# Values projected once and brought by DMA, masks cut to two of three key blocks, and paired score banks in a windowed attention

## The chip, the cores and the metric

The kernel runs on one core of a Trainium2 chip. The metric is the device time of one launch in microseconds (us); less is better. A core has five engines with queues of their own: TensorE (PE, with its weight loads shown apart as PEld), VectorE (DVE), ScalarE (ACT), GpSimd (POOL) and SyncE (SP), which here issues DMAs. Engines wait for each other through semaphores, and each works through its own queue in order.

## The reference, cut to what matters

The input is `x` of 4 x 1024 tokens with 128 features, in float32. Two adaLN blocks follow each other. Block 0 is a linear attention and a mixture of 16 experts. Block 1 begins with the attention that is changed here, and ends with two layers of local attention (8 heads of 64) with a gated MLP.

```python
# block 1, first attention: 16 heads of 8, window 64, 16 prefix keys
qkv = x @ w_qkv.T; q, k, v = split(qkv)          # heads of 8
sg = einsum(q, k[:16]) * scale                    # global prefix keys, causal
st = einsum(q, k_window) * scale                  # keys in (q_pos-64, q_pos], without the prefix
scores = concat(where(mg, sg, -1e9), where(mt, st, -1e9))
out = softmax(scores) @ concat(v[:16], v_window)
x = x + ga * (out @ w_out.T)
# block 0, the experts that are touched too
h = silu(xf @ w1) * (xf @ w3);  y = einsum(h, w2, comb)
```

## The kernel before, in words

Tokens are worked on feature-major: `hT[b]` holds the normed input of batch `b` as 128 features x 1024 tokens. Three stages follow each other: block 0 (to about 316 us of the profile), the windowed attention (316 to 577 us), and the two local layers (577 us to the end). PE runs in the order in which the program writes its matmuls; the order on DVE, ACT and POOL is made by a scheduler when the program is built, and each of them then follows its list. The program divides PSUM into eight banks of 512 floats per partition: four with the tag `s`, two with `t`, one with `m`, one with `o`.

The windowed attention takes 32 tiles of 128 queries (4 batches x 8). A tile is four chunks of 32 queries; each chunk has three blocks of 32 keys (its own and the two before it) and 16 prefix keys, so 112 keys for each of 16 heads. The heads go in four groups `j` of four.

- `scores(b, t)` (L249) fills four `s` banks, one for each `j`: a matmul of an identity with the mask table opens each bank (L255, 448 columns), 16 matmuls add the window's scores (L261), four add the prefix keys (L270). Float32 matmuls run as two instructions, so L261 has 32 for a tile and L270 has 8.
- `weights(b, t)` (L715): for each `j` a maximum (`maximum`, L279 on DVE); for `j` = 0, 1, 2 DVE subtracts it (L724) and ACT takes the exponential (L725); for `j` = 3 four ACT instructions read the bank with the maximum as bias (L728).
- `flip(b, t, js)` (L730) transposes the weights of two `j` on PE into the two `t` banks (L735); ACT copies them out (L737).
- `values(b, t)` (L694): POOL lays the windows of `hT` side by side (L701 to L707), PE projects the values of each of the four chunks' 112 keys (L710, 8 instructions into the `m` bank), and ACT copies them out (L713).
- `outputs(b, t)` (L741) multiplies weights and values into the bank `obank` (L752, 128 instructions); DVE divides by the sum (L754, L756). `back` (L759) turns the result on PE (L762) into the free end of `obank`, and ACT copies it (L765).
- `project_out` (L767), `queries` (L220), `keys` (L228), `tokens` and `normed` (the norms before and after, L773 and L782) come in some tiles only, and use the `m` bank.

One loop over `g` from -1 to 33 holds the written order. For one `g`:

```python
when(g + 2, scores)
when(g + 2, weights)
# queries (b+1) at t = 2, 4; tokens or normed in some g
when(g - 1, back)
when(g + 1, flip, (0, 1)); when(g + 1, values)
when(g, outputs); when(g + 1, flip, (2, 3))
# project_out at g % 4 == 1; keys (b+1) at t = 3, 5; project (first local layer) in the last six
```

All weights of the local layers and the rotary table are loaded at the stage's start (L606 to L615). In block 0, `hidden` (L483) makes two matmuls into two `s` banks, ACT's Silu reads the first (L492), POOL multiplies by the routing weight (L494), DVE multiplies with the second (L496).

Of the kernel before, what the change touches and what calls it, by code (L numbers as in the profile page):

```python
# [19 lines left out]
F32 = mybir.dt.float32  # L20
BF16 = mybir.dt.bfloat16
AF = mybir.ActivationFunctionType
# [4 lines left out]
P = 128  # L27
# [21 lines left out]
def adaln_blocks(ctx: ExitStack, tc: tile.TileContext, a: dict, out: bass.AP):  # L49
# [199 lines left out]
    def scores(b, t):  # L249
        nt = f"{b}_{t}"  # L250
        q1, kx, kg = kept1[b, "q"], kept1[b, "kx"], kept1[b, "kg"]
        S = [ps.tile([P, 512], F32, tag="s", name=f"s_{nt}_{j}", bufs=4) for j in range(4)]
        sv = [x[:, 0 : 4 * (W3 + PREFIX)].rearrange("p (h k) -> p h k", h=4) for x in S]
        for j in range(4):
            pe.matmul(sv[j], lhsT=identb, rhs=mks[:, min(t, 1), :].unsqueeze(1).to_broadcast([P, 4, W3 + PREFIX]), start=True, stop=False)  # L255
        for a in range(4):
            i = 4 * t + a
            lo = max(0, 2 - i)
            for j in range(4):
                rw = slice(32 * j, 32 * j + 32)  # L260
                pe.matmul(  # L261
                    sv[j][32 * a : 32 * a + 32, :, lo * KB : W3].rearrange("p h (c k) -> p h c k", k=KB),
                    lhsT=q1[rw, i * KB : (i + 1) * KB],
                    rhs=kx[rw, i - 2 + lo : i + 1].rearrange("p c h k -> p h c k"),
                    start=False,
                    stop=False,
                )
        for j in range(4):
            rw = slice(32 * j, 32 * j + 32)
            pe.matmul(sv[j][:, :, W3:], lhsT=q1[rw, t * P : (t + 1) * P], rhs=kg[rw, 4 * j : 4 * j + 4, :], start=False, stop=True)  # L270
        mx = pre.tile([P, H0], F32, tag="mx", name=f"mx_{nt}", bufs=3)
        kept1[b, t, "s"] = sv, mx
        if (b, t) == (0, 0):
            for j in range(4):
                maximum(b, t, j)

    def maximum(b, t, j):
        sv, mx = kept1[b, t, "s"]
        dve.tensor_reduce(mx[:, 4 * j : 4 * j + 4], sv[j], AX.X, ALU.max, negate=True)  # L279

    s_attn = float((8.0**0.5) ** -0.25)
    gabo = const("gabo", [P, B])
    with (
# [12 lines left out]
        def blk(k):  # L298
            return slice(k * BLK, (k + 1) * BLK)
# [170 lines left out]
        def shared_hidden(b):  # L470

            hh = []
            for i in range(2):
                h = ps.tile([P, BLK], F32, tag="s", name=f"hs{i}_{b}", bufs=4)
                for k in range(NB):
                    pe.matmul(h[k * INTER : (k + 1) * INTER, :], lhsT=ws13[:, i, :], rhs=hT[b][:, blk(k)], start=True, stop=True)
                hh.append(h)
            u = wp.tile([P, BLK], F32, tag="u", name=f"us_{b}")
            act.activation(u, hh[0], AF.Silu)
            g = kept[b, "gs"] = wb.tile([P, BLK], F32, tag="gs", name=f"gs_{b}")  # L480
            dve.tensor_tensor(g, u, hh[1], ALU.mult)

        def hidden(b, k, c):  # L483

            nm = f"{b}_{k}_{c}"
            hh = []
            for w in (w1, w3):
                h = ps.tile([P, BLK], F32, tag="s", name=f"h_{nm}", bufs=4)
                pe.matmul(h, lhsT=w[:, c * P : (c + 1) * P], rhs=hT[b][:, blk(k)], start=True, stop=True)  # L489
                hh.append(h)  # L490
            u = wp.tile([P, BLK], F32, tag="u", name=f"u_{nm}")
            act.activation(u, hh[0], AF.Silu)  # L492
            kept["u"] = u
            pool.tensor_tensor(u, u, kept[b, k, "cw"][:, c, :], ALU.mult)  # L494
            g = kept[b, k, c, "g"] = wp.tile([P, BLK], F32, tag="g", name=f"g_{nm}", bufs=4)
            dve.tensor_tensor(g, u, hh[1], ALU.mult)  # L496

# [104 lines left out]

    wl = []
    for l in range(DEPTH):
        w = [const1(f"wqkv_{l}", [P, 3, HEADS * DH]), const1(f"wo_{l}", [P, 4, D]), const1(f"w1_{l}", [P, 2 * HID]), const1(f"w2_{l}", [P, 3, D])]
        nc.sync.dma_start(out=w[0], in_=a["wqkv"][l].rearrange("p (i c) -> p i c", i=3))  # L606
        nc.sync.dma_start(out=w[1], in_=a["wo"][l].rearrange("(c p) d -> p c d", p=P))
        nc.sync.dma_start(out=w[2], in_=a["mw1"][l])
        for j, r in enumerate(CH):
            nc.sync.dma_start(out=w[3][:r, j, :], in_=a["mw2"][l][j * P : j * P + r, :])  # L610
        wl.append(w)

    abs_ = [const1(f"ab_{l}", [P, 2, NT, 2, DH]) for l in range(DEPTH)]
    tab = abs_[DEPTH - 1]
    nc.sync.dma_start(out=tab, in_=a["tab"])  # L615

# [68 lines left out]
    m = mods[1]  # L685
    with (
        tc.tile_pool(name="w6o", bufs=1) as wo6,
        tc.tile_pool(name="w6b", bufs=2) as wb,
        tc.tile_pool(name="w6", bufs=3) as wp,
        tc.manual_schedule(engines={mybir.EngineType.PE}),  # L690
    ):
        odd.append(wo6)

        def values(b, t):  # L694

            nt = f"{b}_{t}"
            hr = wp.tile([P, 4, KV], F32, tag="hr", name=f"hr_{nt}", bufs=2)
            c0 = 2 if t == 0 else 0
            win = hT[b][:, (4 * t + c0 - 2) * KB :]
            win = bass.AP(tensor=win.tensor, offset=win.offset, ap=[win.ap[0], [KB, 4 - c0], [1, W3]])  # L700
            pool.tensor_copy(hr[:, c0:, 0:W3], win)  # L701
            if t == 0:

                pool.memset(hr[:, 0:2, 0 : 2 * KB], 0.0)
                pool.tensor_copy(hr[:, 0, 2 * KB : W3], hT[b][:, 0:KB])
                pool.tensor_copy(hr[:, 1, KB:W3], hT[b][:, 0 : 2 * KB])
            pool.tensor_copy(hr[:, :, W3:], hT[b][:, 0:PREFIX].unsqueeze(1).to_broadcast([P, 4, PREFIX]))  # L707
            vp = ps.tile([P, 4, D], F32, tag="m", name=f"vp_{nt}")[0:KV]
            for c in range(4):
                pe.matmul(vp[:, c, :], lhsT=hr[:, c, :], rhs=wqkv1[:, 2, :], start=True, stop=True)  # L710
            v = kept1[b, t, "v"] = wp.tile([KV, 4 * H0, 9], F32, tag="vb", name=f"vb_{nt}")
            pool.memset(v[:, :, 8:9], 1.0)
            act.copy(v[:, :, 0:8], vp.rearrange("p c (h e) -> p (c h) e", e=8))  # L713

        def weights(b, t):  # L715

            sv, mx = kept1[b, t, "s"]
            for j in range(4):
                if (b, t) != (0, 0):
                    maximum(b, t, j)  # L720
                mj = mx[:, 4 * j : 4 * j + 4]
                pr = kept1[b, t, "pr", j] = wp.tile([P, 4, KV], F32, tag="pr", name=f"pr_{b}_{t}_{j}", bufs=8)
                if j < 3:
                    dve.tensor_tensor(pr, sv[j], bc(mj, [P, 4, KV]), ALU.add)  # L724
                    act.activation(pr, pr, AF.Exp)  # L725
                else:
                    for h in range(4):
                        act.activation(pr[:, h, :], sv[j][:, h, :], AF.Exp, bias=mj[:, h : h + 1])  # L728

        def flip(b, t, js):  # L730
            for j in js:
                pr = kept1.pop((b, t, "pr", j))
                tp = ps.tile([P, 4, P], F32, tag="t", name=f"ptr_{b}_{t}_{j}", bufs=2)[0:KV]
                for h in range(4):
                    pe.transpose(tp[:, h, :], pr[:, h, :], ident)  # L735
                pt = kept1[b, t, "p", j] = wp.tile([KV, 4, P], F32, tag="pt", name=f"pt_{b}_{t}_{j}", bufs=8)
                act.copy(pt, tp)  # L737
# [3 lines left out]
        def outputs(b, t):  # L741
# [4 lines left out]
            v = kept1.pop((b, t, "v"))  # L746
            for j in range(4):
                pt = kept1.pop((b, t, "p", j))
                for h in range(4):
                    for c in range(4):  # L750
                        qs = slice(c * KB, (c + 1) * KB)
                        pe.matmul(o[qs, 4 * j + h, :], lhsT=pt[:, h, qs], rhs=v[:, H0 * c + 4 * j + h, :], start=True, stop=True)  # L752
            rs = wp.tile([P, H0, 1], F32, tag="rs", name=f"rs_{b}_{t}")
# [5 lines left out]
        def back(b, t):  # L759

            tp, on = obank[0][:, BLK - P :], kept1.pop((b, t, "o"))
            pe.transpose(tp, on.rearrange("p h e -> p (h e)"), ident)  # L762
# [31 lines left out]
        for g in range(-1, NG8 + 2):  # L794
# [4 lines left out]
            when(g + 2, scores)  # L799
            when(g + 2, weights)  # L800
            if ahead and t in (2, 4):
                queries(b + 1, t // 2 - 1)
# [3 lines left out]
            for at, k, f in ((1, 0, tokens), (3, 0, normed), (5, 1, tokens), (7, 1, normed)):  # L806
                if g == at:
                    f(B - 1, k, "h2")
            when(g - 1, back)
            when(g + 1, flip, (0, 1))  # L810
            when(g + 1, values)
            when(g, outputs)
            when(g + 1, flip, (2, 3))
            if t == 5 and 0 < b <= DEPTH:
# [409 lines left out]
```

## Time and profile before

| | |
|---|---|
| median of 3 runs | 1242.51 us (1238.51 to 1245.01) |
| the profiled execution | 1246.33 us, its span 1244.5 us |
| busy PE, DVE, ACT, POOL | 1162.8, 878.8, 817.8, 823.3 us |
| windowed attention, 316 to 577 us | 261 us |
| its 25 tiles of steady work, 338.9 to 529.4 us | 190.5 us, PE busy 183.22, DVE 127.83, ACT 140.56, POOL 83.34 |
| block 0's experts, 72 to 316 us | 244 us, PE busy 227.81 |

Busy times are unions of an engine's instructions. The windows view gives them for a stretch of the span, counted in us from its start. The timeline gives start and length of merged instructions; the distance from one group's start to the next is what the group costs its engine, since the printed lengths overlap. In brackets stands the idle time before a group and whose end released it.

### The profile page before, as it was taken

The numbers are of one execution on the slowest core, as the hardware profiler recorded it, in microseconds if no ns is written. First come the engines' busy times: TensorE is split into PE (matmuls) and PEld (weight loads), VectorE is DVE, ScalarE is ACT, GpSimd is POOL, SyncE is SP. The second block draws the span as 40 slices with busy tenths as digits, with TensorE's granted clock in tenths as the row PEclk, the third lists the DMA queues.
The fourth block names the chain that finished last, engine by engine and source line by source line (L and its number), as shares of the span: only waits on it lengthen the run. The fifth ranks groups of instructions, "written<-read, shape, count | busy, mean of one in ns | idle before, by whom it ended". The sixth has DMA issues, their size and how long they took to land.

```text
span 1244.5 us, 34772 instructions
## 1 busy us (share of the span) xinstructions
PE 1162.8 (93%) x13578; PEld 714.7 (57%) x13578; DVE 878.8 (71%) x2798; ACT 817.8 (66%) x2223; POOL 823.3 (66%) x813
## 2 busy tenths in 40 slices
PE   6789999999899999988898999999999999999998
PEld 5644453534476667755665556665555556565564
DVE  5556263452476667666878988898898888998864
ACT  3363373322577677766886788788877887788862
POOL 4436445746334445444889988888899889888840
PEclk8699999999999999999999999999999999999999
DMA  6040404021400000000112111111111111111110
GB/s 179 1 130 8 138 0 132 7 74 63 137 4 4 3 20 14 11 3 3 35 27 48 27 35 26 32 40 27 39 28 34 39 29 45 38 27 31 36 40 26
DMA packets 36136, 51.04 MB, mean 41 GB/s; under 512 B 5850, under 2 KB 17668, under 8 KB 35844
## 3 DMA queue, kind: packets, MB, share of 16 engines
q1 hardware_dynamic: 35540, 48.29, 14.1%
q8 instruction: 107, 1.75, 0.6%
q10 hardware_dynamic: 432, 0.53, 0.1%
q14 instruction: 57, 0.47, 0.1%
HBM read 26.52 MB, written 2.36 MB: 23 GB/s over the span
## 4 chain that ended last, share of the span: by engine, by line
PE 43%; DVE 27%; ACT 18%; POOL 7%; issue 5%; DMA 1%; POOLq 0%; ACTq 0%; SPq 0%; DVEq 0%
ACT pr L904 5%; PE h L489 4%; PE yp L951 4%; DVE pr L892 3%; DVE co L658 3%; PE s L885 3%; DVE si L663 3%; DVE ss L665 3%; PE ptr L735 3%; PE qk L653 3%; POOL u L494 2%; ACT sq L656 2%; PE s L261 2%; PE obank L752 2%; DVE ge L997 2%
## 5 line engine op out<-in xcount | busy, mean ns | idle before, releaser
L904 ACT ACTIVATE pr<-pr,mx 128x128 f32<-128x128 f32 x512 | 200.8, 403 | 88.2 <-DVE mx L892 88.1
L673 POOL TENSOR_TENSOR co<-co,si 128x512 f32<-128x512 f32 x123 | 156.7, 1280 | 79.5 <-DVE si L663 72.2
L669 POOL TENSOR_TENSOR ss<-ss,nhalf 128x16 f32<-128x16 f32 x64 | 191.7, 2995 | 5.3
L892 DVE CUSTOM_DVE_ANT_0 pr<-s,masks,ss 128x128 f32<-128x128 f32 x512 | 144.2, 342 | 42.4 <-PE s L885 42.0
L653 PE MATMUL qk<-wqkv,hs 128*128 128x512 f32 x256 | 137.7, 620 | 4.9 <-ACT pt L737 4.9
L494 POOL TENSOR_TENSOR u<-u,cw 128x512 f32<-128x512 f32 x64 | 81.1, 1271 | 74.4 <-ACT u L492 74.4
L489 PE MATMUL h<-hT,w 128*128 128x512 f32 x256 | 123.8, 605 | 4.0 <-DVE g L496 4.0
L496 DVE TENSOR_TENSOR g<-u,h 128x512 f32<-128x512 f32 x64 | 43.8, 686 | 114.9 <-POOL u L494 114.9
L279 DVE TENSOR_REDUCE mx<-s 128x4 f32<-128x448 f32 x128 | 73.5, 617 | 56.4 <-PE s L270 56.4
L658 DVE TENSOR_TENSOR co<-qk,ab 128x512 f32<-128x512 f32 x128 | 86.7, 677 | 26.0 <-ACT sq L656 26.0
L904 ACT ACTIVATION_READ_ACCUMULATOR pr<-pr,mx 128x1 f32 x512 | 101.7, 199 | 0.0
L492 ACT ACTIVATE u<-h 128x512 f32<-128x512 f32 x64 | 38.2, 598 | 93.2 <-PE h L489 85.7
L926 PEld LDWEIGHTS ptr<-ident,pr 128*128 128x128 f32 x512 | 63.5, 141 | 61.6 <-issue 54.8
L663 DVE TENSOR_TENSOR si<-qk,ab 128x512 f32<-128x512 f32 x128 | 86.8, 678 | 0.0
L489 PEld LDWEIGHTS h<-hT,w 128*128 128x128 f32 x256 | 48.3, 194 | 66.2 <-issue 51.0
L665 DVE TENSOR_REDUCE ss<-sq 128x8 f32<-128x512 f32 x128 | 86.2, 673 | 0.0
L656 ACT ACTIVATE sq<-qk 128x512 f32<-128x512 f32 x128 | 74.9, 586 | 14.8 <-PE qk L653 12.3
L845 PE MATMUL qktr<-ident,co 128*128 128x128 f32 x492 | 76.9, 280 | 6.6 <-POOL co L675 5.3
L885 PEld LDWEIGHTS s<-kT,qT 64*64 64x64 f32 x2048 | 56.8, 134 | 45.6 <-issue 22.1
L919 POOL TENSOR_TENSOR pr<-pr,sm 128x512 f32<-128x512 f32 x64 | 74.7, 1168 | 7.9 <-DVE sm L912 7.9
L885 PE MATMUL s<-kT,qT 64*64 64x128 f32 x2048 | 72.1, 277 | 7.6 <-DVE kT L858 6.1
L737 ACT COPY pt<-ptr 112x512 f32<-112x512 f32 x128 | 72.5, 612 | 8.6 <-PE ptr L735 8.6
(212 smaller groups left out, 2871.2 us busy)
## 6 DMA issues: line engine op xcount, KB each, us to landing
cw<-cd SPq DMA_DIRECT2D x128, 128.0 KB, 3.0
ve<-vs SPq DMA_DIRECT2D x120, 128.0 KB, 2.3
hs<-hT SPq DMA_DIRECT2D x16, 256.0 KB, 3.2
out<-out SPq DMA_DIRECT2D x7, 256.0 KB, 2.7
xin<-in_x SPq DMA_DIRECT2D x3, 512.0 KB, 6.1
w<-in_w SPq DMA_DIRECT2D x3, 512.0 KB, 5.0
wqkv<-in_wqkv SPq DMA_DIRECT2D x2, 768.0 KB, 5.3
ab<-in_tab SPq DMA_DIRECT2D x1, 1024.0 KB, 7.3
```

The costliest lines, as they stand in the source:

```text
L489: pe.matmul(h, lhsT=w[:, c * P : (c + 1) * P], rhs=hT[b][:, blk(k)], start=True, stop=True)
L494: pool.tensor_tensor(u, u, kept[b, k, "cw"][:, c, :], ALU.mult)
L653: pe.matmul(ps, lhsT=hs[l, b][:, t * P : (t + 1) * P], rhs=wl[l][0][:, w, :], start=True, stop=True)
L656: act.activation(sq, ph, AF.Square)
L658: dve.tensor_tensor(co, ph, abs_[l][:, 0, t, w, :].unsqueeze(1).to_broadcast([P, HEADS, DH]), ALU.mult)
L663: dve.tensor_tensor(si.rearrange("p h (i e) -> p h i e", i=2), ex, sn, ALU.mult)
L665: dve.tensor_reduce(ss[:, w, :], sq, AX.X, ALU.add)
L669: pool.tensor_tensor(ss, ss, nhalf[:, 0:2].unsqueeze(2).to_broadcast([P, 2, HEADS]), ALU.pow)
L673: pool.tensor_tensor(co, co, si, ALU.add)
L885: pe.matmul(S[j][qs, c, :], lhsT=q[rw, c, qs], rhs=k[rw, c, at : at + P], start=True, stop=True)
L892: dve.tensor_tensor_reduce(out=pr[:, c, :], in0=S[j][:, c, :], in1=mk[:, min(t, 1), :], scale=kept[l, b, t, "ss"][:, 0, h : h + 1], scalar ...
L904: act.activation(pr[:, c, :], pr[:, c, :], AF.Exp, bias=mx[:, j, c : c + 1], scale=-1.0, accum_out=sm[:, j, c : c + 1])
```

## The change

- `values` projects the tile's 128 tokens once (one matmul, two instructions, 128 columns) into a half of an `m` bank. ACT copies the result to `vt`, a DMA writes it to a DRAM tensor `dv` of the batch (whose first 64 rows are zeros), and two DMAs bring the four windows and the prefix rows back as `vb`. It runs two tiles ahead.
- `back` turns the outputs into another part of the same `m` bank that the next `values` uses (columns 128 to 255, the values columns 0 to 127).
- The mask matmul of all tiles but the first of a batch covers two of the three key blocks: 256 columns in place of 448. The middle block, where every key is allowed, and the prefix columns get none.
- Scores lie in two tiles of two banks. A maximum takes 8 heads; the subtraction and exponential of `j` = 0 and 1 are one instruction each of 896 columns (`prw`); `j` = 2 stays apart, `j` = 3 stays on ACT. The order is `j` = 2, 3 and then 0, 1.
- The written order in the loop becomes scores, weights, outputs, flip (3, 2), queries/tokens/normed, back, values, flip (0, 1).
- The local layers' 18 loads are spread over the tiles, one after each tile's window DMA.
- In block 0, `hidden` and `shared_hidden` use one tile of two banks for both matmuls.

```diff
 def scores(b, t):
-    S = [ps.tile([P, 512], F32, tag="s", name=f"s_{nt}_{j}", bufs=4) for j in range(4)]
-    for j in range(4):
-        pe.matmul(sv[j], lhsT=identb, rhs=mks[:, min(t, 1), :].unsqueeze(1).to_broadcast([P, 4, W3 + PREFIX]), start=True, stop=False)
+    S = [ps.tile([P, 2, 512], F32, tag="s", name=f"s_{nt}_{i}", bufs=2) for i in range(2)]
+    for j in (2, 3, 0, 1):
+        to, of = sv[j], mks[:, min(t, 1), :]
+        if t == 0:
+            of = of.unsqueeze(1).to_broadcast([P, 4, KV])
+        else:
+            to = to[:, :, 0:W3].rearrange("p h (c k) -> p h c k", k=KB)[:, :, 0:3:2, :]
+            of = of[:, 0:W3].rearrange("p (c k) -> p c k", k=KB)[:, 0:3:2, :].unsqueeze(1).to_broadcast([P, 4, 2, KB])
+        pe.matmul(to, lhsT=identb, rhs=of, start=True, stop=False)
...
 def hidden(b, k, c):
-    for w in (w1, w3):
-        h = ps.tile([P, BLK], F32, tag="s", name=f"h_{nm}", bufs=4)
-        pe.matmul(h, lhsT=w[:, c * P : (c + 1) * P], rhs=hT[b][:, blk(k)], start=True, stop=True)
+    hh = ps.tile([P, 2, BLK], F32, tag="s", name=f"h_{nm}", bufs=2)
+    for i, w in enumerate((w1, w3)):
+        pe.matmul(hh[:, i], lhsT=w[:, c * P : (c + 1) * P], rhs=hT[b][:, blk(k)], start=True, stop=True)
...
 def values(b, t):
-    hr = wp.tile([P, 4, KV], F32, tag="hr", name=f"hr_{nt}", bufs=2)
-    pool.tensor_copy(hr[:, c0:, 0:W3], win)
...
-    for c in range(4):
-        pe.matmul(vp[:, c, :], lhsT=hr[:, c, :], rhs=wqkv1[:, 2, :], start=True, stop=True)
-    act.copy(v[:, :, 0:8], vp.rearrange("p c (h e) -> p (c h) e", e=8))
+    vp = kept1["bank"][:, 0:D]
+    pe.matmul(vp, lhsT=hT[b][:, t * P : (t + 1) * P], rhs=wqkv1[:, 2, :], start=True, stop=True)
+    act.copy(vt[:, :, 0:8], vp.rearrange("p (h e) -> p h e", e=8))
+    nc.sync.dma_start(out=dv[at : at + P], in_=vt.rearrange("p h e -> p (h e)"))
+    kept1["brought"] = nc.sync.dma_start(out=v[0:W3], in_=win)
+    nc.sync.dma_start(out=v[W3:KV], in_=dv[2 * KB : 2 * KB + PREFIX].unsqueeze(1).to_broadcast([PREFIX, 4, H0 * 9]))
...
 def weights(b, t):
+    for i in (1, 0):
+        maximum(b, t, i)
+        if i == 0:
+            dve.tensor_tensor(wide, sp[0], bc(mi, [P, 2, 4, KV]), ALU.add)
+            act.activation(wide, wide, AF.Exp)
+            continue
+        for h in range(4):
+            act.activation(pr[1][:, h, :], sp[1][:, 1, h, :], AF.Exp, bias=mi[:, 1, h : h + 1])
+        dve.tensor_tensor(pr[0], sp[1][:, 0], bc(mi[:, 0], [P, 4, KV]), ALU.add)
+        act.activation(pr[0], pr[0], AF.Exp)
...
 def back(b, t):
-    tp, on = obank[0][:, BLK - P :], kept1.pop((b, t, "o"))
+    kept1["bank"] = ps.tile([P, BLK], F32, tag="m", name=f"otr1_{b}_{t}")
+    tp, on = kept1["bank"][:, D : 2 * D], kept1.pop((b, t, "o"))
...
     when(g + 2, scores)
     when(g + 2, weights)
+    when(g, outputs)
+    when(g + 1, flip, (3, 2))
...
     when(g - 1, back)
+    for i in {-1: (0, 1)}.get(g, (g + 2,)):
+        when(i, values)
     when(g + 1, flip, (0, 1))
-    when(g + 1, values)
-    when(g, outputs)
-    when(g + 1, flip, (2, 3))
+    if g > 0 and local_loads:
+        with tc.issue_after(kept1["brought"].ins):
+            nc.sync.dma_start(out=local_loads[0][0], in_=local_loads[0][1])
```

## The prediction

> **What bounds it now.** First the page, for engines and stages, then the windows view, which takes one stage out of the average.
>
> ```profile
> PE 1162.8 (93%) x13578; PEld 714.7 (57%) x13578; DVE 878.8 (71%) x2798; ACT 817.8 (66%) x2223; POOL 823.3 (66%) x813
> ```
>
> The steady part of the attention that is changed (length, then PE, PEld, DVE, ACT, POOL, granted clock, DMA share, GB/s):
>
> ```profile
> 338.90:529.40 190.50, 183.22 (x5020) 133.04 (x5019) 127.83 (x301) 140.56 (x350) 83.34 (x148) 1.00 0.04 9
> ```
>
> PE is busy 96% of 25 tiles, 7.62 us a tile; ACT has 5.6 and DVE 5.1. The timeline shows what PE does in a tile without extras (start, length, instruction, operands, count):
>
> ```profile
> 449.06 0.92 PE L255 MATMUL s<-cb,identb 128*128 128x448 bf16 x4
> 449.91 0.93 PE L261 MATMUL s<-kx,q 32*32 32x384 f32 x32
> 450.76 0.47 PE L270 MATMUL s<-kg,q 32*128 32x64 f32 x8
> 451.16 0.33 PE L762 MATMUL obank<-ident,on 128*128 128x128 f32 x1
> 451.33 1.04 PE L735 MATMUL ptr<-ident,pr 128*112 128x128 f32 x8
> 452.20 1.04 PE L710 MATMUL vp<-wqkv,hr 128*112 128x128 f32 x8
> 453.17 1.26 PE L752 MATMUL obank<-vb,pt 112*32 112x9 f32 x128
> 454.35 1.09 PE L735 MATMUL ptr<-ident,pr 128*112 128x128 f32 x8
> 455.28 0.73 PE L255 MATMUL s<-cb,identb 128*128 128x448 bf16 x3
> ```
>
> The same stretch of DVE and of ACT:
>
> ```profile
> 451.23 1.16 DVE L279 TENSOR_REDUCE mx<-s 128x4 f32<-128x448 f32 x2 [1.91 <-PE s L270]
> ...
> 454.61 0.84 ACT L728 ACTIVATE pr<-s,mx 128x112 f32<-128x112 f32 x3
> ...
> 455.80 0.36 ACT L728 ACTIVATE pr<-s,mx 128x112 f32<-128x112 f32 x1
> ```
>
> Start to start, PE's groups cost: masks 0.85, window 0.85, prefix 0.40, turned outputs 0.17, flips 0.87, values 0.97, outputs 1.18, flips 0.93: 6.22 us, without a gap. DVE idles 1.91 us before its maxima. So PE is the bound here, and DVE and ACT have slack because PE has other work between the scores and the next tile's masks.
>
> **PE's work.** Values fall from 8 instructions to 2: 0.97 to 0.24, -0.73 us for 32 tiles. Masks go from 448 to 256 columns in 28 tiles: 0.85 becomes between 0.49 (in proportion to the columns) and 0.85; I take 0.53. A plain tile would need 5.2 us of PE. If PE stayed the bound, 32 x 0.73 + 28 x 0.32 = 32 us would go.
>
> **What takes its place.** The built order of the after program puts a wait into PE's queue twice: the turned outputs wait until the reader of the `m` bank's last use is done (ACT's copy in queries, tokens and normed tiles), and the one values matmul waits for ACT's copy `os` of the turned outputs, since both now share a bank. Behind that matmul are queued the flips (0, 1), the next tile's masks and its window scores. And ACT's order is: four exponentials of `j` = 3, two `pt` copies, the exponential of `j` = 2, the copy of the extra (if any), the wide exponential, `os`. In tiles without an ACT extra `os` stands before the wide exponential. So a tile becomes a loop through three engines. From the first prefix matmul:
>
> - to the end of the first maximum: L270 to L279 is 450.76 to 451.23, 0.47; the maximum now needs four of the eight instructions, 0.57. It takes 896 columns: 0.615 for 448, and from 128 columns (0.288, L756) to 448 (0.615, L724) each costs 1.02 ns, so 1.08. With 0.05 to ACT: 1.70.
> - ACT: four exponentials at 0.24 (three in 0.84, one alone 0.38): 0.96; two copies at 0.50: 1.00; the next exponential 0.50 (its subtraction ends at 3.47, in time); the extra's copy 0.50 (0.70 for a normed tile's 0.78); the wide exponential 0.80 (0.50, and 448 more columns at 0.64 ns, from 0.378 for 112 to 0.593 for 448); `os` 0.26 and 0.05 to PE.
> - PE: values 0.24, flips 0.87, masks 0.53, window 0.86.
>
> Sum with a queries or tokens extra: 1.70 + 0.96 + 1.00 + 0.50 + 0.50 + 0.80 + 0.31 + 0.24 + 0.87 + 0.53 + 0.86 = 8.27 us. Normed 8.47. Plain, without extra and wide exponential: 6.97. The other PE work (outputs 1.18, flips 0.87, the extra 0.96 or 0.49) lies in the loop's shade, and so does what was saved: the loop holds 0.24 + 0.53 of PE's changed work alone.
>
> More tiles: the output projection waits for `vt`'s copy, which follows the wide exponential (5.6), then 0.86: 7.9. Keys add 0.86: 9.13 after tokens, 9.33 after normed. Normed with projection and keys: 8.47 + 0.86, 1.0 until DVE has read the projection (0.75, plus 0.26 of matmul tail), 0.1, 0.86: 11.2. The 25 steady tiles are 2 plain, 3 with projection, 10 queries or tokens, 4 normed, 2 and 1 with keys, 3 with all: 13.9 + 23.7 + 82.7 + 33.9 + 18.3 + 9.3 + 33.6 = 215.4, against 190.5: **+25 us**. Bounds: each row carries about 0.05 us and the wide operations, which no trace row shows, lie between 0.53 (no cost for the second half) and 1.2 (two halves): -0.5 to +0.5 a tile, +12 to +38.
>
> A rule of the Trainium skill bears on this. The trace shows such a wait once: of `os`, 0.8 us, since `obank` held both outputs and turned outputs.
>
> ```profile
>   PE obank L752: 0.8, 1
> ```
>
> "PSUM — Partial Sum Buffer", section "PSUM bank collisions raise a hardware error", says to guard PSUM by bank and quadrant, not by address. By it the values must wait for `os` though their columns differ, which is the sum above; were the guard by address, a tile with an extra would lose the 0.80 and 0.31 but for 0.24, about -0.87, a plain one -1.1, and the steady part would end at +4.
>
> **The other parts.**
> - Paired banks for scores: the masks of `j` = 0, 1 wait for the wide subtraction, which ends 4.5 us after the prefix matmul; PE comes there at 5.6 or later. Free; without that cover the loop through DVE alone would be 4.5 + 0.27 + 0.86 = 5.6.
> - Value DMAs: `cd` issued at 70.67 lets `cw` go at 72.63, and `cw` lands in 1.6 to 3.4, so about 5 us. `outputs` needs them two tiles later, over 10 us after `vt`. SP waits inside, but behind it stand only the next values' DMAs and the local loads, needed from tile 11 on. Zero; exposed, it would cost the missing microseconds in each tile.
> - POOL loses the window copies (0.50 + 0.24 a tile). It waited for PE there; nothing is gained.
> - Stage start: `j` = 3 first lets PE open the second tile's scores 1.4 us earlier, and I take -1.5; the first values' DMA chain (0 to +5) could eat it.
> - Stage end, six tiles with a local projection: it waits for a `pt` copy as before (1.25 us in the first), but DVE's three passes over it (2.0 us) now meet the maxima: +3, between 0 and +6.
> - Block 0: the first of two matmuls can no longer start when Silu has freed a bank; it waits for DVE's product two units before. In the timeline four units' second matmul waited for that product already, so up to 0.86 each; other cases end in a wait for routing. Against it, ACT loads two tables fewer (1.28 each) ahead of a copy for which PE waited 1.75. I take +0.5, between -2.6 and +5.
>
> Sum: 25 - 1.5 + 3 + 0.5 = +27 us. The profiled execution took 1246.33 (span 1244.5, the rest around it), so 1273; the median, 0.3% lower, 1242.5 + 27 = **1269.5**.
>
> **Rivals.**
> 1. PE stays the bound: ACT's `os` ends before PE comes to the values, and 32 us go: 1210. For it: PE is 96% busy and ACT 74%. Against: PE comes there 2.6 us (plain) or 3.4 us (queries) after the prefix matmul, and ACT's own work from the maximum puts `os` at 4.4 or 5.75. It decides when ACT's chain is under 6 us less 1.97 of PE behind it, less than half of its rows. 0.08.
> 2. The waits are there but about half as long (ACT's rows overlap more than start to start shows): +5, 1247. 0.10.
> 3. The clock falls. After 2.3 us without PE work (wait for the routing, 121.6 to 123.9) the granted clock of this stretch was 0.91:
>
> ```profile
> 110.00:130.00 20.00, 17.21 (x45) 7.50 (x45) 13.77 (x49) 3.94 (x7) 8.64 (x7) 0.91 0.06 17
> ```
>
> In a queries tile PE would idle 1.4 and 0.9 us, with 0.1 of work between. At half clock the 2.5 us of PE in the loop double; in half of the 25 tiles that is +30: 1300. Against: gaps up to 1.8 us (75.8, 668.6) left the clock at 1.00 in their rows. 0.12.
>
> **Numbers.** The forecast has 0.70. The range goes from 1244, where rival 2 still lies mostly inside, to 1300, half of rival 3; rival 1, the other halves and the forecast's edges are the 2 in 10 outside. About 0.5% (6 us) is what a measurement can tell here: faster 0.09, same 0.08, slower 0.83.
>
> **What would show it.** Mask groups of queries tiles 8.3 us apart in place of 7.15, plain ones 7.0; PE busy near 75% of the stage; values matmuls idle before them, released by `os`, and turned outputs released by the copies of queries, tokens and normed. Wrong: tiles under 6.5 us; or waits on the value DMAs ahead of `outputs`; or a granted clock under 0.95 in the stage. The local layers should last as before, 667 us.

## The result, and the profile after

The changed kernel takes 1316.49 us (median of 4 runs, 1310.58 to 1325.8) against 1241.49 before, a ratio of 1.0609 with a 95% interval of 1.0556 to 1.0661. It is slower, as forecast, by 75 us where 27 were forecast, and lies 16 us above the range. The profiled execution took 1314.51 us, with a span of 1312.7, 68.2 longer than that of the kernel before; the stages below add up to these 68.2. In the sessions of the runs below, the kernel before took 1241.5 to 1245.6 us, so medians of different runs compare to some 4 us; each ratio is against the kernel before in the run's own session.

The busy line of the page after:

```profile
PE 1169.1 (89%) x13386; PEld 710.9 (54%) x13386; DVE 872.1 (66%) x2702; ACT 805.8 (61%) x2189; POOL 797.6 (61%) x738
```

PE has fewer matmuls and is busy for longer. The windows view tells why (first the steady part, tile 3's masks to tile 28's, then the stage's start and its end; the last three columns are the granted clock, DMA's share and GB/s):

```profile
340.33:591.54 251.21, 188.62 (x4870) 130.48 (x4867) 122.41 (x224) 135.73 (x324) 63.07 (x90) 0.88 0.20 57
316.86:340.30 23.44, 16.98 (x309) 9.83 (x308) 12.96 (x16) 13.16 (x30) 7.17 (x12) 1.00 0.14 38
591.54:645.00 53.46, 41.27 (x1062) 27.13 (x1060) 29.89 (x55) 27.16 (x62) 16.99 (x15) 0.87 0.11 31
```

The steady part went from 190.5 us at a granted clock of 1.00 to 251.2 at 0.88. DVE and ACT have 5 us less work in it than before, so neither became a bound by its work. PE idles 62.6 us (7.3 before). And for 57.8 us of the steady part the clock's records show a granted clock of 0.50, called half clock below; PE worked in 53.0 of them, and what it does there takes up to twice the time. The clock of 0.88 is also under the 0.95 that the prediction named as a sign of being wrong. By stages, in the profiled executions:

| us | before | after |
|---|---|---|
| to the first masks of the attention | 315.6 | 316.9 |
| its first three tiles | 23.3 | 23.5 |
| 25 steady tiles | 190.5 | 251.2 |
| from tile 28's masks to the first matmul of `turn`, which begins the local layers | 49.9 | 56.1 |
| the rest, local layers | 665.3 | 665.1 |

PE's waits in the steady part (total us, count, longest):

```profile
PE otr L713 <- ACT os L781: 20.6, 25, 1.7
PE otr L778 <- ACT hT L161: 11.8, 7, 1.8
PE otr L778 <- ACT xt_h L795: 10.6, 7, 1.6
PE obank L767 <- issue: 7.0, 5, 2.4
PE otr L778 <- ACT q L226: 6.2, 6, 1.5
```

These are the two waits of the forecast: the values matmul (L713) waits for `os` in every tile, the turned outputs (L778) wait for ACT's reader of normed, tokens and queries. Their place in one queries tile at full clock, PE alone:

```profile
531.50 0.47 PE L279 MATMUL s<-kg,q 32*128 32x64 f32 x8
531.90 1.26 PE L767 MATMUL obank<-vb,pt 112*32 112x9 f32 x128
533.09 1.08 PE L750 MATMUL ptr<-ident,pr 128*112 128x128 f32 x8
534.01 1.02 PE L225 MATMUL qp<-hT,wqkv 128*128 128x512 f32 x2
536.24 0.33 PE L778 MATMUL otr<-ident,on 128*128 128x128 f32 x1 [1.20 <-ACT q L226]
537.23 0.49 PE L713 MATMUL otr<-wqkv,hT 128*128 128x128 f32 x2 [0.66 <-ACT os L781]
537.55 1.04 PE L750 MATMUL ptr<-ident,prw 128*112 128x128 f32 x8
538.43 0.60 PE L263 MATMUL s<-cb,identb 128*128 128x256 bf16 x4
```

From 535.0 to 537.2 PE does 0.33 us of work. The values stand 5.73 us after the prefix matmul; the forecast's chain had them at 5.77.

### The profile page after: what moved, and what is told of

The parts are those of the page before. It is cut to its first block, busy times and chain, and to the rows that moved or that the text cites. A ratio compares the mean times of both kernels' runs of the same rounds, so it can differ in the third digit from the quotient of the medians.

```text
span 1312.7 us, 34270 instructions
## 1 busy us (share of the span) xinstructions
PE 1169.1 (89%) x13386; PEld 710.9 (54%) x13386; DVE 872.1 (66%) x2702; ACT 805.8 (61%) x2189; POOL 797.6 (61%) x738
## 4 chain that ended last, share of the span: by engine, by line
PE 19%; DVE 18%; ACT 12%; POOL 2%; issue 1%; DMA 0%; DVEq 0%; ACTq 0%; POOLq 0%
ACT pr L926 4%; PE yp L973 4%; DVE pr L914 3%; PE s L907 3%; DVE co L663 3%; DVE si L668 3%; DVE ss L670 3%; PE qk L658 2%; DVE ge L1019 2%; ACT sq L661 2%; PE o L962 2%; PE qktr L867 1%; ACT ge L1012 1%; PE v L886 1%; DVE kT L880 1%; PE gm L1008 1%
## 5 line engine op out<-in xcount | busy, mean ns | idle before, releaser
L678 POOL TENSOR_TENSOR co<-co,si 128x512 f32<-128x512 f32 x123 | 156.6, 1278 | 83.7 <-DVE si L668 76.6
L290 DVE TENSOR_REDUCE mx<-s 128x8 f32<-128x896 f32 x64 | 66.8, 1085 | 94.0 <-PE s L279 93.9
L715 POOL MEMSET vt<- 128x16 f32 x32 | 3.9, 126 | 169.1 <-DMA dv<-vt 166.7
L739 ACT ACTIVATE pr<-s,mx 128x112 f32<-128x112 f32 x128 | 34.8, 354 | 95.8 <-DVE mx L290 95.2
```

The costliest lines, as they stand in the source:

```text
L678: pool.tensor_tensor(co, co, si, ALU.add)
```

## The experiments

### Is it the clock?

`e1_filled` puts matmuls that nothing reads where PE waits, into a bank of the flips.

```diff
+    if 0 <= g - 1 < NG8:
+        fill = ps.tile([P, BLK], F32, tag="t", name=f"fill_{g}", bufs=2)
+        pe.matmul(fill, lhsT=wqkv1[:, 0, :], rhs=hT[0][:, 0:BLK], start=True, stop=True)
     when(g - 1, back)
+    if 0 <= g - 1 < NG8:
+        pe.matmul(fill[:, 0 : 2 * P], lhsT=wqkv1[:, 0, :], rhs=hT[0][:, 0 : 2 * P], start=True, stop=True)
```

> The changed kernel, with work added that nothing reads: in each tile a matmul of 512 columns (two instructions, 0.86 us) after the queries, tokens or normed matmuls, ahead of the turned outputs, and one of 256 columns (0.4 us) behind the turned outputs, ahead of the values. Both lie where PE waits 1.2 to 1.8 and 0.7 us. Theory 1, the clock: the waits let the granted clock fall to 0.50 in 58 of the 251 us of the steady part, and PE loses 26 us by it; with PE busy in them the clock stays at 1.00 and the time falls by about 25, to 1290, though PE does 1.26 us more in a tile. Theory 2, the loop alone: the half clock lies in the shade of ACT and DVE, and nothing is gained: 1316 to 1325, the filled waits being a little longer than the old ones.

Measured: 1292.84 us (ratio to before 1.036, 1.0328 to 1.0393): 24 us less than the changed kernel by the medians, 31 by the ratios, though PE does more. Its steady part in the windows view:

```profile
343.10:574.40 231.30, 202.01 (x4968) 133.30 (x4969) 122.58 (x224) 135.20 (x324) 63.35 (x89) 0.99 0.22 62
```

The clock is at 0.99, and the time at half clock in the steady part falls from 57.8 to 6.8 us. Theory 1 holds.

`e16_small_fill` keeps only 256 columns ahead of the turned outputs.

```diff
+    if 0 <= g - 1 < NG8:
+        fill = ps.tile([P, BLK], F32, tag="t", name=f"fill_{g}", bufs=2)
+        pe.matmul(fill[:, 0 : 2 * P], lhsT=wqkv1[:, 0, :], rhs=hT[0][:, 0 : 2 * P], start=True, stop=True)
     when(g - 1, back)
```

> The changed kernel with a matmul of 256 columns (0.4 us) that nothing reads ahead of the turned outputs, a third of the work that was filled in before, and none behind them. Theory 1, the clock goes by PE's busy share in slots of 3.41 us (in the traces so far almost all slots with a share up to 0.5 were followed by half the clock, and nearly none above 0.53): 0.4 us in a tile of 8.4 lifts some of these slots over the bound, so the half clock falls from 58 us of the steady part to 25 to 45, and the time to 1298 to 1310. Theory 2, the length of the longest wait decides: the waits ahead of the turned outputs go from 1.2 to 1.8 down to 0.8 to 1.4, and nearly all of the half clock goes: 1290 to 1295.

Measured: 1305.98 us (1.0504, 1.0442 to 1.0566).

```profile
339.90:583.90 244.00, 196.69 (x4919) 137.19 (x4917) 122.41 (x224) 136.12 (x324) 62.97 (x89) 0.92 0.22 58
```

The time at half clock is 41.0 us, both numbers as theory 1 had them: a third of the fill takes away a third of what the whole fill did. The waits ahead of the turned outputs are at most 0.9 us now (up to 1.8 before the fill), and most of the falls stayed, so a wait's length doesn't decide. What tells them better is read from the clock's records: the clock is granted in slots of 3.41 us (in the changed kernel every spell at half clock in the stage lasts 3.41, 6.83 or 10.24). From 316 to 640 us of ten traces (the kernels before and after, `e1_filled`, `e2_own_bank`, `e3_loads_first`, `e10_all_old_order_spread`, `e12_back_first`, `e14_os_on_dve`, `e15_values_last`, `e16_small_fill`), the slots at full clock by PE's busy share in them:

| busy share of a slot | slots | followed by half clock |
|---|---|---|
| under 0.45 | 56 | 55 |
| 0.45 to 0.50 | 30 | 22 |
| 0.50 to 0.55 | 48 | 15 |
| 0.55 to 0.60 | 23 | 4 |
| above 0.60 | 656 | 9 |

By the longest wait within the slot the same slots are far less clear: of 53 with 1.25 to 1.5 us, 23 were followed by half clock. So the share of a slot tells it, with the turn near one half. Five more traces of the old order agree above 0.60 (1 of 410 slots followed by half clock) and less well under 0.45 (8 of 12); `e13_fine` stands apart, as shown below. The Trainium skill, "TensorE: Matmul & The Clock Gate", section "HAM oscillation — how this bites in real kernels", gives the rule "no PE-idle gaps >~3.4µs"; here no wait in the steady part of the changed kernel was longer than 2.5 us, and the clock fell in it all the same. The measurement decides.

### Is it the shared bank?

`e2_own_bank` turns the outputs into `obank` again and leaves the values the `m` bank.

```diff
-    kept1["bank"] = ps.tile([P, BLK], F32, tag="m", name=f"otr1_{b}_{t}")
-    tp, on = kept1["bank"][:, D : 2 * D], kept1.pop((b, t, "o"))
+    tp, on = obank[0][:, BLK - P :], kept1.pop((b, t, "o"))
```

> The changed kernel, but the turned outputs go to the free end of obank as before, and the values have the m bank for themselves. Theory 1, the shared bank: the values wait no longer for os behind the wide exponential, nor the turned outputs for the reader of the m bank's last use; the loop loses 0.87 to 1.1 us in each of 25 tiles, so 1290, and with fewer waits the clock falls less often, so 1265 to 1290. Theory 2, the order of the loop: PE comes to the values before ACT has read the m bank's queries, tokens or normed, the wait only moves from one matmul to the next, and 5 to 10 us go: 1305 to 1311.

Measured: 1286.29 us (1.0313, 1.0276 to 1.035), 30 us better; theory 1's size. Its steady part is 36.7 us shorter: PE idles 15.8 us less, and works 16.4 us at half clock in place of 53.0, which is worth up to 18.3. Its waits show that part of one bank's wait was changed for another's:

```profile
PE obank L777 <- DVE on L771: 31.0, 22, 2.1
```

The turned outputs of the tile before now wait for DVE's division of the outputs just written, which lie in other columns of the same bank. `e12_back_first` therefore writes them ahead of the outputs as well:

```diff
+    when(g - 1, back)
     when(g, outputs)
     when(g + 1, flip, (3, 2))
...
-    when(g - 1, back)
     for i in {-1: (0, 1)}.get(g, (g + 2,)):
```

> The changed kernel with the turned outputs in obank and their matmul written ahead of the outputs, where it was before; the rest of the changed order stays. With obank alone PE waited 35.2 us in 24 tiles at that matmul, for DVE's division of the outputs just made, which lie in the same bank. Theory 1, a bank is guarded as a whole: that wait goes, 25 to 35 us go: 1250 to 1262. Theory 2: the rest of the order (flip of j = 3, 2 early, values ahead of the flip of j = 0, 1) holds PE at the values or the flips by as much: 1270 to 1286.

Measured: 1275.28 us (1.0245, 1.0205 to 1.0286): in theory 2's range. The wait is at the values, which follow queries, tokens or normed in the `m` bank at once:

```profile
PE vp L713 <- ACT hT L161: 10.4, 7, 1.5
PE obank L767 <- ACT os L780: 8.9, 25, 0.4
PE vp L713 <- ACT xt_h L794: 8.5, 7, 1.3
PE vp L713 <- ACT q L226: 5.3, 6, 1.1
```

`e15_values_last` puts the flip of `j` = 0, 1 between them:

```diff
+    when(g + 1, flip, (0, 1))
     for i in {-1: (0, 1)}.get(g, (g + 2,)):
         when(i, values)
     kept1["bank"] = None
-    when(g + 1, flip, (0, 1))
```

> The changed kernel with the turned outputs in obank, their matmul ahead of the outputs, and the values matmul behind the flip of j = 0, 1 in place of ahead of it. With the values ahead of that flip PE waited there for ACT's reader of the queries, tokens or normed matmuls in the m bank, 24.8 us in 21 tiles, and the time was 1275. Theory 1, that wait is what is left of the order's cost: the flip (0.87 us) lies over it, 15 to 25 us go: 1250 to 1260. Theory 2, the flip of j = 0, 1 then waits itself, for the wide exponential: 1268 to 1278.

Measured: 1285.18 us (1.0317, 1.0277 to 1.0357), worse by 10. Both theories failed. The wait is gone from the values, and part of it is at the next users of the bank:

```profile
PE y L785 <- ACT vt L716: 7.5, 6, 1.5
PE ptr L750 <- ACT pt L752: 5.9, 20, 0.3
...
PE kp L235 <- ACT vt L716: 4.5, 3, 1.5
```

`vt` stands on ACT behind two `pt` copies, and `project_out` and `keys` wait for it. In all, PE idles less in the steady part than in `e12_back_first` (38.3 us, 44.6). What made its steady part 10.9 us longer is the clock: PE worked 37.1 us at half clock, in place of 9.4, which costs up to 13.9 us more.

`e14_os_on_dve` asks whether ACT's wide exponential ahead of `os` is what the values wait for.

```diff
-    act.copy(kept1[b, t // 4, "os"][:, (t % 4) * P : (t % 4 + 1) * P], tp)
+    dve.tensor_copy(kept1[b, t // 4, "os"][:, (t % 4) * P : (t % 4 + 1) * P], tp)
```

> The changed kernel, but DVE copies the turned outputs (os) and not ACT; it stands on DVE directly behind the division that feeds the turned outputs. Theory 1: ACT's wide exponential ahead of os is what the values wait for; in a queries tile of the trace os would end 0.4 us sooner, 10 us in 25 tiles, and with shorter waits the clock falls less often: 1290 to 1306. Theory 2: the turned outputs themselves come late (their wait for the reader of the bank's last use) and the values' wait only moves there: 1310 to 1318.

Measured: 1324.07 us (1.062, 1.0565 to 1.0675), the ratio of the changed kernel. Nothing is gained, and in total the wait is the same with another engine's name:

```profile
PE otr L713 <- DVE os L781: 19.9, 25, 2.3
```

Tile by tile it is not the same. In 14 of the 25, most with queries or normed, the values waited 0.38 us where they had waited 0.5 to 0.7 (once 1.15): the wide exponential had held `os` there, as theory 1 said, by about 0.3 us. In seven tiles with tokens the wait rose from 0.7 to 1.03, since `os` now stands behind the norm's statistics on DVE, and in three tiles without a copy of an extra from 1.6 or 1.7 to between 2.1 and 2.4, behind DVE's wide subtraction. The waits ahead of the turned outputs stayed (28.2 us, 28.6 before), as theory 2 said.

### What are the parts worth in the old order?

`e4_masks_only` takes the masks alone (the `to`, `of` lines of the diff, with the order of `j` as before).

> The kernel before with nothing but the mask matmuls of 256 columns in place of 448 in 28 tiles. Theory 1: PE is the bound, the masks cost 0.53 in place of 0.85, and 28 x 0.32 = 9 us go: 1234 to 1237. Theory 2: what PE saves there it waits for elsewhere (a bank that is not free, DVE): within 3 us of before.

Measured: 1239.37 us (0.9972, 0.9952 to 0.9992), 4 us less, between the theories. `e5_values_spread` takes the new `values` and the spread loads alone.

> The kernel before with values once and by DMA alone (and the spread loads). Theory 1, PE is the bound: 32 x 0.73 = 23 us less, 10 of them given back in stops of PE: 1220 to 1232. Theory 2, with masks cut as well the kernel was at 1245, since the masks waited for ACT's exponentials of j = 3 in their banks and PE stopped for code: the values alone bring 0 to 5: 1238 to 1243.

Measured: 1244.29 us (0.9991, 0.9959 to 1.0024), no change, as theory 2 had it. `e8_masks_values_spread` has both, with four single score banks.

> The kernel before with values once and by DMA, masks in two of three blocks, and the local layers' loads spread over the tiles; four single score banks, the loop's order and the turned outputs in obank as before. Theory 1, PE is the bound: 0.73 x 32 + 0.32 x 28 = 32 us less, of which stops of PE inside the outputs (1 to 2.5 us, some ten of them in the run of the old order, where one wait of 5.6 us on the values' DMA behind the loads stood too) take 10 back: 1220 to 1228. Theory 2, the chain through DVE and ACT is the bound once PE has less to do: 1235 to 1245.

Measured: 1245.29 us (0.9998, 0.9977 to 1.0019): theory 2's number. The windows view of `e5_values_spread`, then the waits of `e8_masks_values_spread`:

```profile
335.20:525.30 190.10, 168.98 (x4869) 117.74 (x4868) 127.48 (x302) 132.57 (x349) 63.69 (x90) 0.99 0.27 75
```

```profile
PE s L261 <- ACT pr L736: 11.5, 16, 1.4
PE obank L760 <- issue: 7.3, 4, 2.3
...
PE ptr L743 <- issue: 2.9, 3, 1.7
```

PE's busy time did fall, by 14 us (183.22 to 168.98), and the steady part stayed at 190 us. With less work in front of them, the masks come before ACT's exponentials have freed the bank of `j` = 3, and PE stops for no releaser. Some of what PE saved also went into half clock: it holds for 13.7 us of the steady part of `e8_masks_values_spread`, 3.4 of that of `e5_values_spread`, none before.

`e9_all_old_order` adds the two-bank scores and the experts' paired banks (loads first), `e10_all_old_order_spread` spreads the loads.

> The kernel before with three parts of the change: values once and by DMA two tiles ahead, masks in two of three blocks, two-bank scores (with the experts' paired banks). Not taken over are the written order of the loop, the order of j, the shared bank and the spread loads. Theory 1, order and shared bank make the loss: the parts are sound by themselves, PE stays the bound or nearly, and 15 to 32 us go against the kernel before: 1210 to 1227. Theory 2, the wide operations and the two-bank scores make the chain through DVE and ACT too long in any order: 1245 or more.

> The same and two-bank scores with wide operations, so the kernel of the old order with its loads spread. Theory 1: the wait of 5.6 us for the first values' DMA goes and nothing else changes: 5 to 7 us below the one with the loads first, 1240. Against the one with four single banks it tells what the wide scores are worth: theory 1, nothing or up to 5 us; theory 2, they cost 10 us or more, as a coarser release holds up masks.

Measured: 1247.09 us (1.0016, 0.9993 to 1.0039) and 1239.14 (0.9972, 0.995 to 0.9994). The steady part of the second:

```profile
339.10:524.90 185.80, 167.34 (x4869) 120.19 (x4870) 123.67 (x224) 130.00 (x321) 63.40 (x89) 0.96 0.28 78
```

The first has theory 2's number, but not for its reason: against `e8_masks_values_spread` the wide scores gain 6 us of the steady part, since the masks' wait of 11.5 us for ACT is 1.2 (for DVE) with them. The second came in at theory 1's number, with the wide scores worth a little more than it allowed. What takes the gain is PE's stops, 10 us in the second's steady part, and half clock, 16.4 us of it. The same parts are 77 us faster here than in the changed kernel's order with its shared bank; no run takes the order of the loop and that of `j` apart. The spread loads are worth about 5 us, all in the first three tiles (28.7 us with the loads first, 23.3 with them spread): with them first, the first values' DMA lies behind them. `e3_loads_first` shows the same in the changed kernel.

```diff
+    for dst, src in local_loads:
+        nc.sync.dma_start(out=dst, in_=src)
+    local_loads = []
```

> The changed kernel, but the 18 loads of the local layers are issued at the stage's start, as before, and not one in each tile. Three times in the steady part PE stops inside the outputs for 1.8 to 2.4 us with no releaser; before it stopped so twice, for 1.1 and 1.4. Theory 1: the loads among the tiles make these stops (or their length): they go back to 1.1 to 1.4, and with the half clock that follows them 5 to 10 us go: 1306 to 1311. Theory 2: the stops have another cause, such as PE's code, and the time stays at 1316 within 4.

Measured: 1328.98 us (1.0658, 1.0621 to 1.0695), against both theories: 12 us more by the medians, 6 by the ratios, whose intervals overlap, and no gain in any case. The stage's first three tiles took 30.0 us in place of 23.5, with this wait:

```profile
PE obank L770 <- DMA vb<-dv: 5.3, 1, 5.3
```

and 76.6 us of the steady part were at half clock (57.8 in the changed kernel). PE's stops of up to 2.5 us stayed, so the loads don't make them.

### What are PE's stops?

One in the changed kernel, ahead of the last 8 output matmuls:

```profile
414.98 1.19 PE L767 MATMUL obank<-vb,pt 112*32 112x9 f32 x120
418.61 0.30 PE L767 MATMUL obank<-vb,pt 112*32 112x9 f32 x8 [2.43 <-issue]
```

In the DMA records a transfer of 16384 bytes of instructions begins at 416.08, just as PE stops at 416.17, and takes 1.16 us; PE goes on 1.36 us after its end. So it is everywhere: in the sixteen traces kept here, PE stops 75 times for over 0.9 us with no releaser between 316 and 600 us, and each of these stops ends 1.2 to 1.6 us after such a transfer has ended, though in the changed kernel, for one, the transfers end 3.3 to 16 us apart. Most transfers (37 of 42 there) come with no such stop. Counted in PE's matmul rows, the stops of the changed kernel, of `e2_own_bank` and of `e14_os_on_dve` stand at the same rows (2369, 2752, 3135, 5688, 6071), at whatever time these come. They lie 383 rows apart or several times a third of that: 383 rows with a weight load each are 766 instructions. `e11_woven` splits the outputs; its edit against `e10_all_old_order_spread`:

```diff
-    when(g, outputs)
-    when(g + 1, flip, (2, 3))
+    when(g, outputs, (0, 1))
+    when(g + 1, flip, (2,))
+    when(g, outputs, (2, 3))
+    when(g + 1, flip, (3,))
```

> The same, but a tile's 128 output matmuls are split: those of j = 0, 1, then the flip of j = 2, those of j = 2, 3, then the flip of j = 3. Theory 1, code: PE runs the 128 short outputs in 1.2 us, faster than a transfer of instructions of 16384 bytes arrives (0.9 to 1.4 us by the trace), and stops where such a transfer falls there; spread over 1.7 us the stops get shorter by 0.4 us each or fewer: 3 to 8 us less than without. Theory 2: the stops have another cause, and nothing changes.

Measured: 1237.65 us (0.9934, 0.9912 to 0.9956), the fastest version here and faster than both kernels, than the one before by under 1%; against `e10_all_old_order_spread` it is 1.5 us, and the two intervals overlap, so theory 1's 3 to 8 us are not shown. The stops inside the outputs are 1.1 to 1.75 us in place of 1.2 to 2.0, but there are more of them: with those in the flips they add up to 10.4 us from 338 to 580 us, 10.6 in `e10_all_old_order_spread`.

`e13_fine` puts the flip's eight transposes singly between groups of eight output matmuls.

> The woven kernel of the old order with the eight transposes of the flip of j = 2, 3 put singly among the last 64 output matmuls, one after every eight. Theory 1, code: the output matmuls take more time in a row, a transfer of instructions is late by less, 3 to 6 us go: 1232 to 1235. Theory 2: the stops only move, 1237 within 3.

Measured: 1283.09 us (1.0305, 1.0255 to 1.0356), against both theories. The stops inside the outputs are gone, PE idles 3.5 us in the whole steady part, and the kernel is 45 us slower than `e11_woven`:

```profile
338.30:557.20 218.90, 215.39 (x4876) 142.68 (x4869) 125.89 (x226) 132.13 (x322) 61.09 (x89) 0.96 0.24 66
```

```profile
456.62 0.32 PE L750 MATMUL ptr<-ident,pr 128*112 128x128 f32 x1
456.87 0.25 PE L771 MATMUL obank<-vb,pt 112*32 112x9 f32 x8
457.05 0.32 PE L750 MATMUL ptr<-ident,pr 128*112 128x128 f32 x1
457.30 0.25 PE L771 MATMUL obank<-vb,pt 112*32 112x9 f32 x8
```

From start to start, a transpose and eight outputs take 0.43 us here; in runs of their own they take 0.12 (0.92 for 8) and 0.07 (1.19 for 128). By this each change of form costs about 0.12 us, an estimate from these rows, and a tile has some sixteen.

Its clock tells more. Of the 58 slots at full clock in its steady part, five were followed by half clock, and PE shows as busy from end to end of all five. They are the five that lie to 95% or more within a tile's alternating stretch (3.45 us); of the other 53, which lie in one to 89% at most, none was followed by half clock. Counted by what the two groups take in runs of their own, 0.19 of each 0.43 us, a slot is 0.47 busy at 95% and 0.50 at 89%. This is an estimate, but it puts the turn near one half again, and would mean that the busy time of the profile hides idle time of PE where the two forms alternate.

That the stops are code arriving late is thus well supported (their end at a fixed time after a transfer, the fixed rows, that they are gone when the outputs take longer). Why most transfers come in time and some don't stays open: no run changed the code's size alone.

## Why the prediction was right or wrong

- **PE's loop through ACT: right, in place and size.** In the queries tile shown, the masks take 0.53 us from start to start (0.53 forecast), the values 0.32 (0.24), and ACT's wide exponential 0.84 (0.80). Undisturbed tiles at full clock, from masks to masks: 8.36 and 8.82 for queries (8.27 forecast), 8.55 for tokens (8.27), 9.17 for tokens with keys (9.13), 11.33 and 11.36 for all extras (11.2). Where no tile after was undisturbed, the filled run gives 8.50 for normed (8.47), 9.36 with keys (9.33), 8.33 for output projection (7.9) and 7.50 for plain (6.97), the last two with the fill in them. With these, and 8.36 for queries, the 25 tiles make 220 us; the forecast had 215.4.
- **What released the values: right.** In the tiles with a copy of an extra, ACT makes `os` directly behind the wide exponential, and the values wait about 0.7 us for it. `e14_os_on_dve` adds that the exponential is worth only 0.3 us of that chain, since the turned outputs come late too.
- **The clock: the step that failed.** It stood as rival 3, with a chance of 0.12, as something else than the forecast, and the argument against it was the length of single waits. But the forecast's own loop makes it: PE idles 1.6 to 4.0 us in each tile (2.5 in the mean), most of it close together, and that leaves slots of 3.41 us under half busy. The sum put the clock at nothing. The price was right in size: +30 in the text; after, PE worked 53 us of the steady part at half clock and lost up to 26.5 by it, and the fill gave 24 back. The two belonged in one sum: 1269.5 + 30 would have been 1299.5, and the rest up to 1316 is in the next two points.
- **PE's stops: not seen.** Five in the steady part make 9.5 us; before, two made 2.5. The trace of before showed both inside the outputs, with no releaser, and the forecast passed over them:

```profile
PE obank L752 <- issue: 3.1, 4, 1.4
```

- **The sum.** Steady part: 25 forecast, 60.7 measured; of it 29.5 are the loop at full clock (220 less 190.5), up to 26.5 the clock and 7.0 the stops; together 2.3 too much, since some of these lie over each other. By PE's own time the 60.7 are 55.3 more of idling and up to 26.5 by half clock, less 21.1 of work that is gone. Stage end: 3 forecast, 6.2 measured, at a clock of 0.87. First tiles: -1.5 forecast, +0.2. Block 0: 0.5 forecast, 1.2.
- **The rivals.** PE staying the bound (1210) did not come even in the old order: the parts saved PE 14 to 17 us of busy time there, and nearly all turned into waits. Its condition also counted 1.97 us of PE behind the values where the sum has 2.50, the masks left out. A wait for the values' DMA beyond the first tiles did not come either.
- **Guarding by bank: right.** The changed kernel waits for `os` in 25 tiles though its columns differ from those of the values, and `e2_own_bank` shows the same in `obank`. In these kernels a bank that is shared so is also one tile of the program, so no run tells whether bank or tile is what is guarded.

## What to carry to other kernels

Before one bank takes a second use, write down who reads it last and where that reader stands in its engine's queue: each user of the `m` bank here waited for ACT's queue, and moving one of them moved part of the wait to the next. When a change lets the engine that sets the pace wait, cost the wait and the fall of its clock together: look at its busy share in each slot of 3.4 us, not at the length of a wait. Where matmuls of two forms alternate, count what they take in runs of one form. And work taken from the bound pays only as far as the next engine is free in that stage: in the old order 14 to 17 us of PE's busy time went, and 0 to 6 us of time.

## What was not expected of the hardware

- PE's clock fell after slots with a busy share under about 0.5, though no wait in the steady part came near a whole slot; work that nothing reads made the kernel 24 us faster. In `e13_fine` it fell after slots that show as wholly busy, all within alternating matmuls.
- PE stopped for 0.9 to 2.7 us in or near groups of very short matmuls (128 in 1.19 us), each time until 1.2 to 1.6 us after a transfer of 16384 bytes of instructions. The Trainium skill, "Runtime: NRT & Kernel Launch", section "Instruction fetch mechanics", says that code comes in such blocks, of 256 instructions (three make 768, beside the 766 above), and that crossing one is mostly hidden. It is not always hidden here, where 256 instructions of the outputs run in about the time of one transfer (0.9 to 1.4 us in the changed kernel).
- Alternating two forms of float32 matmul costs some 0.12 us a change on PE, with no idle time to show for it: the busy time of the steady part rose from 170.51 us to 215.39, some 4 of it by the clock.
